# Attention weights of layer 3: scores computed twice, the second time with keys on partitions, instead of transposing the weights

## The chip, the core and the metric

The kernel runs on one core of a Trainium2 chip. The core has TensorE (PE, matmuls; its weight loads are listed as PEld), VectorE (DVE), ScalarE (ACT), GpSimd (POOL) and SyncE (SP), which here only issues DMAs. Matmul results land in PSUM, eight banks of 128 partitions by 512 fp32 numbers; everything else works from SBUF. The metric is the device time of one execution in microseconds (us), taken as the median of several runs.

## The reference

The program is a chain of four layers on 4 sequences of 512 tokens with 512 channels: a cross-attention (layer 0), two recurrent layers (1 and 2) and a perceiver-like cross-attention with an MLP (layer 3). All arithmetic is fp32. Only layer 3 is changed. There the latents are the output of layer 2, and the keys are the 512 context tokens (some masked) followed by the 512 latents:

```python
h = jnp.concatenate([x, latents], axis=1)          # 512 context tokens, 512 latents
q = (latents @ q_w + q_b).reshape(b, k_len, NH, DH)     # NH 16 heads, DH 32
kv = (h @ kv_w + kv_b).reshape(b, p + k_len, NH, DH, 2)
kmat, v = (kv[..., 0], kv[..., 1])
attn = jnp.einsum('bkhd,bnhd->bhkn', q, kmat) / DH
attn = jnp.where(full_mask[:, None, None, :], attn, -jnp.inf)
attn = jax.nn.softmax(attn.astype(jnp.float32), axis=-1)
attn_out = jnp.einsum('bhkn,bnhd->bkhd', attn, v).reshape(b, k_len, H)
attn_out = attn_out @ out_w + out_b + residual
out = rmsnorm(attn_out, postnorm_w)
out = jax.nn.gelu(out @ mlp_w1 + mlp_b1) @ mlp_w2 + mlp_b2
return out + residual
```

## The kernel before

Layer 3 goes through 4 batches (b). A batch's channels are cut into 4 blocks of 128 (m), and a block holds 4 heads of 32 channels (r). The 512 queries are cut into 4 tiles of 128 (lt). A **group** is (b, m, lt): 128 queries, 4 heads, 1024 keys; there are 64 of them. A **unit** is (b, m), four groups.

- `begin(b)` loads the context, transposed on the host, and the mask, and transposes the latents on TensorE (L1125).
- `prep(b, m)` loads the three weight blocks (L1137) and makes q (L1141, negated and divided by 32), the keys kT (L1148) for context (a = 0) and latents (a = 1), with channels on partitions, and the values v with keys on partitions (L1153). It is cut into five pieces by `yield`.
- `scores(g, a)` (L1169) makes, for one half of the keys and each head, a matmul over 32 channels with the 128 queries on the PSUM partitions and 512 keys along the row. The four heads use four row tiles of the array, so they run beside each other. A VectorE instruction (L1179) adds the mask, writes the scores to SBUF and keeps the least along the row (scores are negated, so this is the largest).
- `weights(g)`: ScalarE takes exp(least - score) and sums it along the row (L1197), VectorE inverts the sum (L1200), GpSimd multiplies the weights by it (L1201).
- `turned` transposes the weights on TensorE, four heads of 128 keys at a time (L1209), and copies them to SBUF, on VectorE for three of eight key blocks (L1212), on ScalarE for five (L1214).
- `values` multiplies v with the turned weights (L1225): 32 output rows per head, so four column tiles of the array beside each other, 128 query columns each. `attended` adds the bias of v (L1242).
- `finish(b)` is the output block of a batch: projection, residual, norm, then the MLP in 32 pieces of `ph` (first matmul and gelu) and `po` (second matmul). It has 38 pieces.

The order on TensorE in layer 3 is the program's order; the order on the other engines is made by the framework's scheduler from the dependences and tiles. The main loop (L1325) issues, for each group, the scores of this group, the transposes and values of the group before, and between them pieces of the next preparation (`early`) and of the output block of the batch before (`rest`). The output block of batch b - 1 starts with the first group of batch b that is turned, so during batch 0 there is none, and that of batch 3 runs alone at the end. PSUM is shared out as four banks for scores and pieces, two for transposes, and one for values.

A tile with a tag and `bufs=n` rotates through n buffers: a new tile waits until the readers and writers of the one n allocations before are done. DMAs on SP are issued in order, so one that waits for its buffer holds up those behind it.

Layer 0, which is not changed, already works in the manner of the new code: scores once for the largest (L242, L254), the largest taken off, scores again with keys on partitions (L279), exponential (L298), values over 512 columns (L304).

Of the kernel before, what the change touches and what calls it, by code (L numbers as in the profile page):

```python
# [30 lines left out]
def tile_xattn_rwkv_perceiver(ctx: ExitStack, tc: tile.TileContext, t: dict, out: bass.AP):  # L31
# [1055 lines left out]
    def layer3():  # L1087
# [4 lines left out]
        with (  # L1092
# [3 lines left out]
            tc.tile_pool(name="l3ps", bufs=4, space=PSUM) as ps_s,  # L1096
            tc.tile_pool(name="l3pt", bufs=2, space=PSUM) as ps_t,
# [5 lines left out]
            vb = cp.tile([P, KC], F32, name="vb")  # L1103
            nc.sync.dma_start(vb, t["L3_vb"].rearrange("(k p) -> p k", p=P))
# [6 lines left out]
            def begin(b):  # L1111

                d = st[b]
                cT = d["cT"] = bp.tile([P, KC, L], F32, tag="cT", name="cT")
                nc.sync.dma_start(cT, t["ctxT"][:, b * L : (b + 1) * L].rearrange("(k p) n -> p k n", p=P))
                mi = bp.tile([P, L], I32, tag="mi", name="mi")
                nc.sync.dma_start(mi, t["mask3"][b : b + 1, :].to_broadcast([P, L]))
                nm = d["nm"] = bp.tile([P, 2, L], F32, tag="nm", name="nm", bufs=2)
                nc.vector.tensor_scalar(nm[:, 0], mi, 0.0, 1e30, ALU.is_equal, ALU.mult)
                nc.gpsimd.memset(nm[:, 1], 0.0)  # L1120
                xT = d["xT"] = bp.tile([P, KC, L], F32, tag="xT", name="xT")
                for k in range(KC):
                    pt = ps_s.tile([P, L], F32, tag="s", name="ptx")
                    for i in range(LT):
                        nc.tensor.transpose(pt[:, i * P : (i + 1) * P], xn[b][i][:, k * P : (k + 1) * P], ident)  # L1125
                    nc.scalar.copy(xT[:, k, :], pt)
                    if k % 2:
                        yield

            def prep(b, m):  # L1130
# [4 lines left out]
                for x in "qkv":  # L1135
                    w3[x] = bp.tile([P, KC, P], F32, tag="w3" + x, name="w3" + x, bufs=2)
                    nc.sync.dma_start(w3[x], t["L3_W" + x][:, ms].rearrange("(k p) n -> p k n", p=P))  # L1137
                q = d["q", m] = bp.tile([P, L], F32, tag="q", name="q", bufs=2)
# [4 lines left out]
                kT = d["k", m] = bp.tile([P, 2, L], F32, tag="kT", name="kT", bufs=2)  # L1143
                v = d["v", m] = bp.tile([P, NB, P], F32, tag="v", name="v", bufs=2)
                for a, src in enumerate((d["cT"], d["xT"])):
                    pm = ps_s.tile([P, L], F32, tag="s", name="pk")
                    mm(pm, [(w3["k"][:, k, :], src[:, k, :]) for k in range(KC)])
                    nc.scalar.activation(kT[:, a, :], pm, AF.Identity, bias=cols[:, m, 1:2])  # L1148
                    yield
                    pm = ps_s.tile([P, LT, P], F32, tag="s", name="pv")  # L1150
                    for j in range(LT):
                        mm(pm[:, j, :], [(src[:, k, j * P : (j + 1) * P], w3["v"][:, k, :]) for k in range(KC)])
                    nc.vector.tensor_copy(v[:, a * LT : (a + 1) * LT, :], pm)  # L1153
                    yield

            def scores(g, a):

                b, m, lt = g
                d = st[b]
                if a == 0:  # L1160
                    d["mx"] = sp.tile([P, 2, NR], F32, tag="mx", name="mx", bufs=3)
                    d["sm"] = sp.tile([P, NR], F32, tag="sm", name="sm", bufs=3)
                    d["sc"] = [sp.tile([P, 2, L], F32, tag="sc", name="sc", bufs=8) for _ in range(NR)]
                mx = d["mx"]
                ps = []
                for r in range(NR):
                    rs = slice(32 * r, 32 * r + 32)
                    psc = ps_s.tile([P, L], F32, tag="s", name="psc")
                    nc.tensor.matmul(  # L1169
                        psc,  # L1170
                        d["q", m][rs, lt * P : (lt + 1) * P],
                        d["k", m][rs, a, :],
                        start=True,
                        stop=True,
                        tile_position=(32 * r, 0),
                    )
                    ps.append(psc)
                for r in range(NR):
                    nc.vector.tensor_tensor_reduce(  # L1179
                        d["sc"][r][:, a, :],  # L1180
                        ps[r],
                        d["nm"][:, a, :],
                        1.0,
                        mx[:, 0, r : r + 1] if a else 3.0e38,
                        ALU.add,
                        ALU.min,
                        mx[:, a, r : r + 1],
                    )

            def weights(g):  # L1190

                d = st[g[0]]
                mx, sm, scs = d["mx"], d["sm"], d["sc"]
                rs = sp.tile([P, NR], F32, tag="rs", name="rs", bufs=3)
                for r in range(NR):
                    sc = scs[r].rearrange("p a l -> p (a l)")
                    nc.scalar.activation(  # L1197
                        sc, sc, AF.Exp, bias=mx[:, 1, r : r + 1], scale=-1.0, accum_out=sm[:, r : r + 1]
                    )
                    nc.vector.reciprocal(rs[:, r : r + 1], sm[:, r : r + 1])  # L1200
                    nc.gpsimd.tensor_scalar(sc, sc, rs[:, r : r + 1], 0.0, ALU.mult, ALU.add)  # L1201
                return scs

            def turned(g, scs, ss, po):

                for s in ss:
                    pt = ps_t.tile([P, NR, P], F32, tag="t", name="pt")
                    for r in range(NR):
                        nc.tensor.transpose(pt[:, r, :], scs[r][:, s // LT, s % LT * P : (s % LT + 1) * P], ident)  # L1209
                    aT = sp.tile([P, NR, P], F32, tag="aT", name="aT", bufs=6)  # L1210
                    if s > 4:
                        nc.vector.tensor_copy(aT, pt)  # L1212
                    else:
                        nc.scalar.copy(aT, pt)  # L1214
                    sums.append((g, s, aT, po))

            sums = []

            def values():

                for g, s, aT, po in sums:
                    b, m, lt = g
                    v = st[b]["v", m]
                    for r in range(NR):
                        nc.tensor.matmul(  # L1225
                            po[32 * r : 32 * r + 32, :],
                            v[:, s, 32 * r : 32 * r + 32],
                            aT[:, r, :],
                            start=(s == 0),
                            stop=(s == NB - 1),  # L1230
                            tile_position=(0, 32 * r),
                        )
                    if s == NB - 1:
                        attended(g, po)
                sums.clear()

            def attended(g, po):
                b, m, lt = g
                d = st[b]
                if "y" not in d:  # L1240
                    d["y"] = bp.tile([P, KC, L], F32, tag="y", name="y")
                nc.scalar.activation(d["y"][:, m, lt * P : (lt + 1) * P], po, AF.Identity, bias=vb[:, m : m + 1])  # L1242

            def finish(b):
# [5 lines left out]
                for lt in range(LT):  # L1250
# [6 lines left out]
                    sq = sp.tile([P, C], F32, tag="sq", name="sq", bufs=1)  # L1257
# [51 lines left out]

# [6 lines left out]

            groups = [(b, m, lt) for b in range(B) for m in range(KC) for lt in range(LT)]
            first = chain(begin(0), prep(0, 0))  # L1320
            for _ in first:
                pass
            early = rest = iter(())
            old = None
            for i, g in enumerate(groups + [None]):  # L1325
                if g and g[2] == 0:
                    for _ in early:
                        pass
                    b, m, _ = g
# [4 lines left out]
                if old and old[0][1:] == (0, 0) and old[0][0] > 0:  # L1334
                    for _ in rest:
                        pass
                    rest = finish(old[0][0] - 1)
                if old:
                    po = ps_o.tile([P, P], F32, tag="o", name="po", bufs=2)
                for a in range(2):  # L1340
                    if g:
                        scores(g, a)
                    values()
                    if old:
                        turned(*old, range(4 * a, 4 * a + 2), po)
                    if piece(early, rest):
                        values()
                    piece(rest)
                    if old:
                        turned(*old, range(4 * a + 2, 4 * a + 4), po)  # L1350
                old = (g, weights(g)) if g else None
            values()
# [81 lines left out]
```

## Time and profile before

| | |
|---|---|
| median of 3 runs | 3876.62 us (3872.99 to 3885.42) |
| the profiled run, its own time | 3879.5 us |
| its span, first to last instruction | 3877.8 us |
| mean granted TensorE clock | 0.962 |
| busy PE, DVE, ACT, POOL over the span | 93%, 65%, 48%, 40% |
| first scores of layer 3 (L1169) | 2446.6 us |
| last attended values (L1242) | start at 3742.3 us |
| matmul records by line: L1169, L1209, L1225 | 1024, 2048, 4096 |

Times in the views count from the span's first instruction. A row of the costliest groups gives line, engine, operation, output <- inputs, shapes, how often (x), then the busy time, the mean duration in ns of one, and the idle time of the engine before them with what ended it. A row of the timeline gives start, duration, engine, line, operation, tiles, shape and number of records merged into it. A row of stretches gives its bounds, its length, the busy time and number of instructions of each engine, the granted clock, the DMA share and GB/s. A matmul's duration contains the passage through the array, in which the next one has already begun.

### The profile page before, as it was taken

The numbers are of one execution on the slowest core, as the hardware profiler recorded it, in microseconds if no ns is written. First come the engines' busy times: TensorE is split into PE (matmuls) and PEld (weight loads), VectorE is DVE, ScalarE is ACT, GpSimd is POOL, SyncE is SP. The second block draws the span as 40 slices with busy tenths as digits, with TensorE's granted clock in tenths as the row PEclk, the third lists the DMA queues.
The fourth block names the chain that finished last, engine by engine and source line by source line (L and its number), as shares of the span: only waits on it lengthen the run. The fifth ranks groups of instructions, "written<-read, shape, count | busy, mean of one in ns | idle before, by whom it ended". The sixth has DMA issues, their size and how long they took to land.

```text
span 3877.8 us, 60788 instructions
## 1 busy us (share of the span) xinstructions
PE 3619.7 (93%) x24256; PEld 2114.2 (55%) x24256; DVE 2526.8 (65%) x4565; ACT 1856.0 (48%) x3178; POOL 1554.1 (40%) x980
## 2 busy tenths in 40 slices
PE   9999999988999999999999976889999999999989
PEld 3333333555556665656665533555666566656656
DVE  6777777589988888888888860455434443443440
ACT  4767676434444444444444422455454445444531
POOL 4777867424444444444444432222221311221220
PEclk9999999989999999999999987999999999999999
DMA  4000000155777777777777745100122112201213
GB/s 148 23 12 23 12 9 20 57 140 131 158 169 175 172 181 175 174 168 172 168 174 174 174 115 142 43 26 15 51 84 71 51 60 88 76 31 68 69 66 124
DMA packets 187115, 386.94 MB, mean 100 GB/s; under 512 B 16528, under 2 KB 43280, under 8 KB 184784
## 3 DMA queue, kind: packets, MB, share of 16 engines
q1 hardware_dynamic: 148528, 251.45, 20.1%
q0 software_dynamic: 38304, 131.61, 18.3%
q8 instruction: 191, 3.13, 0.3%
q14 instruction: 92, 0.75, 0.1%
HBM read 247.23 MB, written 4.19 MB: 65 GB/s over the span
## 4 chain that ended last, share of the span: by engine, by line
PE 70%; DVE 14%; DMA 6%; ACT 4%; issue 3%; POOL 3%; SPq 0%; POOLq 0%; DVEq 0%; ACTq 0%
PE pm L73 10%; PE pt L1209 6%; PE pv L73 6%; PE po L73 6%; PE ph L73 6%; DMA kv<-A 5%; PE psc L242 4%; PE pst L279 4%; PE psc L1169 4%; PE po L1225 3%; PE pr L73 3%; PE po L304 3%; DVE ry L867 3%; PE pk L73 3%; DVE kv L862 2%
## 5 line engine op out<-in xcount | busy, mean ns | idle before, releaser
L1201 POOL TENSOR_SCALAR sc<-sc,rs 128x1024 f32<-128x1024 f32 x256 | 288.5, 1129 | 931.6 <-DVE rs L1200 916.0
L292 POOL TENSOR_TENSOR aT<-aT,nmT 128x1536 f32<-128x1536 f32 x124 | 428.8, 3462 | 205.7 <-ACT aT L290 182.5
L254 DVE CUSTOM_DVE_ANT_0 sc<-psc,nm 128x512 f32<-128x512 f32 x512 | 354.0, 691 | 147.6 <-PE psc L242 89.9
L867 DVE TENSOR_TENSOR ry<-kv,o_r 128x1024 f32<-128x1024 f32 x256 | 350.3, 1408 | 3.4
L1209 PE MATMUL pt<-ident,sc 128*128 128x128 f32 x2048 | 285.1, 284 | 36.2 <-ACT aT L1214 36.2
L1197 ACT ACTIVATE sc<-sc,mx 128x1024 f32<-128x1024 f32 x256 | 291.9, 1142 | 38.1 <-DVE mx L1179 34.3
L862 DVE TENSOR_TENSOR_SCAN kv<-W,kv 128x1032 f32<-128x1032 f32 x128 | 295.8, 2311 | 0.0
L1179 DVE CUSTOM_DVE_ANT_0 sc<-psc,nm,mx 128x512 f32<-128x512 f32 x256 | 179.6, 746 | 171.3 <-PE psc L1169 171.3
L1214 ACT COPY aT<-pt 128x512 f32<-128x512 f32 x320 | 173.9, 584 | 241.2 <-PE pt L1209 241.0
L1209 PEld LDWEIGHTS pt<-ident,sc 128*128 128x128 f32 x2048 | 233.2, 144 | 101.6 <-issue 54.4
L290 ACT COPY aT<-pst 128x512 f32<-128x512 f32 x372 | 196.5, 595 | 177.1 <-PE pst L279 176.6
L584 POOL DMA_DIRECT2D kv<-A x127 | 119.1, 938 | 377.0 <-DVE kv L839 373.9
L298 ACT ACTIVATE aT<-aT 128x2048 f32<-128x2048 f32 x128 | 246.7, 1929 | 5.6 <-POOL aT L292 4.8
L73 PE MATMUL po<-l_m,hT 128*128 128x512 f32 x512 | 236.9, 608 | 4.4 <-ACT hT L1295 4.4
L73 PE MATMUL ph<-nT,l_m 128*128 128x256 f32 x1024 | 235.4, 384 | 0.0
L1304 DVE TENSOR_TENSOR x<-po,x 128x512 f32<-128x512 f32 x64 | 44.1, 689 | 265.3 <-PE po L73 265.3
L279 PE MATMUL pst<-q,km 32*128 32x512 f32 x1024 | 206.2, 639 | 9.4 <-DVE mxs L254 5.8
L73 PEld LDWEIGHTS ph<-nT,l_m 128*128 128x128 f32 x1024 | 191.8, 191 | 34.2 <-issue 9.9
L833 DVE TENSOR_TENSOR A<-vr,o_k 128x1024 f32<-128x1024 f32 x128 | 155.5, 1215 | 80.7 <-DMA kv<-A 80.6
L242 PE MATMUL psc<-km,q 32*128 32x512 f32 x1024 | 198.2, 651 | 0.8 <-ACT q L223 0.8
L929 POOL TENSOR_TENSOR gn_rs<-gn_rs,mhalf 128x64 f32<-128x64 f32 x16 | 186.4, 11648 | 21.7 <-DVE gn_rs L927 21.7
L881 PE MATMUL py<-ry,k 128*32 128x512 f32 x1024 | 157.8, 631 | 38.7 <-DVE ry L867 27.3
(257 smaller groups left out, 7153.1 us busy)
## 6 DMA issues: line engine op xcount, KB each, us to landing
l_m<-in_L_W SPq DMA_DIRECT2D x64, 1024.0 KB, 5.1
kv<-A POOLq DMA_DIRECT2D x127, 516.0 KB, 7.4
L_wk<-in_L_Wk SPq DMA_DIRECT2D x16, 1024.0 KB, 7.5
L_wr<-in_L_Wr SPq DMA_DIRECT2D x16, 1024.0 KB, 7.6
L_wv<-in_L_Wv SPq DMA_DIRECT2D x16, 1024.0 KB, 5.8
L_wg<-in_L_Wg SPq DMA_DIRECT2D x16, 1024.0 KB, 7.9
L_wo<-in_L_Wo SPq DMA_DIRECT2D x64, 256.0 KB, 6.9
L_fk<-in_L_fWk SPq DMA_DIRECT2D x16, 1024.0 KB, 8.9
```

Source lines behind the costliest of these rows:

```text
L73: nc.tensor.matmul(ps, lhsT, rhs, start=(i == 0), stop=(i == len(pairs) - 1))
L242: nc.tensor.matmul(psc, d["q"][g][rs, lt * P : (lt + 1) * P], d["km"][rs, a, :], start=True, stop=True, tile_position=(32 * r, 0),)
L254: nc.vector.tensor_tensor_reduce(sc, ps[r], d["nm"][lt], 1.0, -3.0e38, ALU.add, ALU.max, mxs[:, a, lt, c : c + 1])
L279: nc.tensor.matmul(pst, d["km"][rs, a, s * P : (s + 1) * P], d["q2", a][rs, :], start=True, stop=True, tile_position=(32 * r, 0),)
L290: nc.scalar.copy(w[:, r, :], pst)
L292: nc.gpsimd.tensor_tensor(w[:, n:, :], w[:, n:, :], nmT[:, None, :].to_broadcast([P, NR - n, L]), ALU.add)
L298: nc.scalar.activation(w, w, AF.Exp)
L862: nc.vector.tensor_tensor_scan(flat(kv), flat(W[g % 2]), flat(kv), 0.0, ALU.mult, ALU.add)
L867: nc.vector.tensor_tensor(y, kv[:, 4 * h : 4 * h + 4, None, :TP].to_broadcast([P, 4, 2, TP]), d["r"][:, i].rearrange("p (o m) -> p o m", o ...
L1197: nc.scalar.activation(sc, sc, AF.Exp, bias=mx[:, 1, r : r + 1], scale=-1.0, accum_out=sm[:, r : r + 1])
L1201: nc.gpsimd.tensor_scalar(sc, sc, rs[:, r : r + 1], 0.0, ALU.mult, ALU.add)
L1209: nc.tensor.transpose(pt[:, r, :], scs[r][:, s // LT, s % LT * P : (s % LT + 1) * P], ident)
```

## The change

Scores are made twice. `least` does the first pass as before, but keeps only the least of each row; the scores go to a scratch tile that nobody reads. When all four query tiles of a unit are through, `spread` transposes the column of least values, broadcast to 128 columns, so that each lands along the row on all partitions, and ScalarE copies it to `mb`. `turned` makes the scores again with operands exchanged: 128 keys on partitions, all 512 queries along the row. VectorE subtracts `mb` (it adds no mask), ScalarE takes the exponential of four heads at once, with the mask as a bias per partition. GpSimd adds the eight weight tiles of a unit up in `acc`; `counted` multiplies `acc` by ones, which sums over keys and repeats the sum on the 32 rows of the head, and VectorE inverts it. `values` works on 512 query columns; its result is copied to y, and `divided` multiplies it by the inverted sum. The bias of v is added to v itself.

```diff
-            tc.tile_pool(name="l3ps", bufs=4, space=PSUM) as ps_s,
-            tc.tile_pool(name="l3pt", bufs=2, space=PSUM) as ps_t,
+            tc.tile_pool(name="l3ps", bufs=7, space=PSUM) as ps_s,
...
-                mi = bp.tile([P, L], I32, tag="mi", name="mi")
+                mi = sp.tile([P, L], I32, tag="sc", name="mi")
                 nc.sync.dma_start(mi, t["mask3"][b : b + 1, :].to_broadcast([P, L]))
...
+                mci = bp.tile([P, LT], I32, tag="mci", name="mci", bufs=2)
+                nc.sync.dma_start(mci, t["mask3"][b].rearrange("(s p) -> p s", p=P))
+                mc = d["mc"] = bp.tile([P, LT], F32, tag="mc", name="mc", bufs=2)
+                nc.vector.tensor_scalar(mc, mci, 0.0, -1e30, ALU.is_equal, ALU.mult)
...
-                    w3[x] = bp.tile([P, KC, P], F32, tag="w3" + x, name="w3" + x, bufs=2)
+                    w3[x] = bp.tile([P, KC, P], F32, tag="w3" + x, name="w3" + x)
...
+            def row_scores(lhsT, rhs, name):
+                ps = []
                 for r in range(NR):
                     rs = slice(32 * r, 32 * r + 32)
+                    psc = ps_s.tile([P, L], F32, tag="s", name=name)
+                    nc.tensor.matmul(psc, lhsT[rs], rhs[rs], start=True, stop=True, tile_position=(32 * r, 0))
                     ps.append(psc)
+                return ps
...
+                ps = row_scores(d["q", m][:, lt * P : (lt + 1) * P], d["k", m][:, a, :], "psc")
                 for r in range(NR):
+                    sc = sp.tile([P, L], F32, tag="sc", name="sc", bufs=2)
                     nc.vector.tensor_tensor_reduce(
...
+            def spread(u):
+                b, m = u
+                d = st[b]
+                mb = d["mb"] = sp.tile([P, NR, L], F32, tag="mb", name="mb", bufs=1)
                 for r in range(NR):
+                    pb = ps_s.tile([P, L], F32, tag="s", name="pb")
+                    for lt in range(LT):
+                        nc.tensor.transpose(
+                            pb[:, lt * P : (lt + 1) * P], d["mx", m][:, 1, lt, r : r + 1].to_broadcast([P, P]), ident
                         )
+                    nc.scalar.copy(mb[:, r, :], pb)
+
+            def turned(u, s):
+                b, m = u
+                d = st[b]
+                ps = row_scores(d["k", m][:, s // LT, s % LT * P : (s % LT + 1) * P], d["q", m], "pst")
+                w = d["w", s] = sp.tile([P, NR, L], F32, tag="aT", name="aT", bufs=3)
+                for r in range(NR):
+                    nc.vector.tensor_tensor(w[:, r, :], ps[r], d["mb"][:, r, :], ALU.subtract)
+                wf = w.rearrange("p r l -> p (r l)")
+                if s < LT:
+                    nc.scalar.activation(wf, wf, AF.Exp, bias=d["mc"][:, s : s + 1], scale=-1.0)
+                else:
+                    nc.scalar.activation(wf, wf, AF.Exp, scale=-1.0)
+                if s == 1:
+                    acc = d["acc", m] = sp.tile([P, NR, L], F32, tag="acc", name="acc", bufs=1)
+                    nc.gpsimd.tensor_tensor(acc, d["w", 0], w, ALU.add)
+                elif s > 1:
+                    nc.gpsimd.tensor_tensor(d["acc", m], d["acc", m], w, ALU.add)
...
+            def counted(u):
+                b, m = u
+                d = st[b]
+                pn = ps_s.tile([P, L], F32, tag="s", name="pn")
+                columns(pn, lambda r: ones, d["acc", m], start=True, stop=True)
+                rs = d["rs", m] = sp.tile([P, L], F32, tag="sc", name="rs")
+                nc.vector.reciprocal(rs, pn)
+
+            def divided(u):
+                b, m = u
+                d = st[b]
+                y = d["y"][:, m, :]
+                nc.vector.tensor_tensor(y, y, d["rs", m], ALU.mult)
```

`columns` is the loop over four heads with column tiles that `values` had. The squares' scratch in `finish` (sq) moves to the tag sc as well. The loop runs over 138 steps, eight to a unit: in a step stand one `least` (of 8) of unit n, one `turned` (of 8) of unit n - 1, and one `values`, two steps behind its `turned`:

```diff
+            LAG = 2
...
+                w, ws = divmod(i - NB - LAG, NB)
...
+                if u:
+                    least(u, s // 2, s % 2)
+                if piece(early):
+                    pass
+                elif piece(rest):
+                    left -= 1
                 if old:
+                    if s == 0:
+                        spread(old)
+                if ws == NB - 1 and 0 <= w < len(units):
+                    counted(units[w])
+                if old:
+                    turned(old, s)
+                if left > min(34, behind(i)) and piece(rest):
+                    left -= 1
+                if 0 <= w < len(units):
+                    values(units[w], ws)
+                    if ws == NB - 1:
+                        divided(units[w])
```

A step takes a piece of the next preparation if there is one, else one of the output block; `behind(i)` says how many output pieces may still be left at step i, so that the 38 pieces are spread over the 32 steps of the next batch. An output block starts when its batch's first following unit reaches `values` (steps 42, 74 and 106).

## The prediction

> **What bounds the kernel now.** I read the page's row of 40 slices first, then the stretches of layer 3, then TensorE's order in time. Layer 3's first scores start at 2446.6 us; the last copy of attended values (L1242) is at 3742.3, and the 136 us after it, to the end at 3877.8, are the last batch's output block, which the diff hardly touches. So the change plays in 1296 us. Those I cut at 2707, where batch 0's attention ends: until then no output block of an earlier batch exists to fill gaps.
>
> ```profile
> 2446.60:2707.00 260.40, 234.69 (x2211) 149.53 (x2211) 139.55 (x403) 137.79 (x251) 76.92 (x69) 0.95 0.07 21
> 2707.00:3742.60 1035.60, 1006.10 (x7626) 646.46 (x7625) 446.08 (x1223) 508.15 (x883) 234.15 (x213) 0.98 0.19 64
> ```
>
> Columns: stretch, length, then busy time of PE, PEld, DVE, ACT, POOL, then the granted clock, DMA share and GB/s. PE is busy 97% of the second stretch and 90% of the first; VectorE (DVE) 43% and 54%. A busy PE can still wait inside its matmuls, so what a matmul run costs is read from the distance to the next run's start:
>
> ```profile
> 3161.89 1.04 PE L1209 MATMUL pt<-ident,sc 128*128 128x128 f32 x8
> 3162.86 1.25 PE L1169 MATMUL psc<-kT,q 32*128 32x512 f32 x8
> ...
> 2571.84 1.14 PE L1169 MATMUL psc<-kT,q 32*128 32x512 f32 x8
> 2572.91 0.65 PE L1225 MATMUL po<-aT,v 128*32 128x128 f32 x16
> 2573.49 1.09 PE L1209 MATMUL pt<-ident,sc 128*128 128x128 f32 x8
> ...
> 326.32 1.34 PE L279 MATMUL pst<-q,km 32*128 32x512 f32 x8
> 327.60 1.06 PE L304 MATMUL po<-aT,vp 128*32 128x512 f32 x8
> 328.59 1.14 PE L242 MATMUL psc<-km,q 32*128 32x512 f32 x8
> ```
>
> Each line is a run: start, length, line, tiles, records (two for an fp32 matmul, one for a transpose). Costs by distance: four head scores (8 records) 1.07 us, eight transposes 0.97, two value steps (16 records of 128 columns) 0.57. The last three lines are layer 0, which already works as the new code will: values over 512 columns (8 records) cost 1.00, scores with keys on partitions 1.28 here and 1.07 where nothing waits (the shortest of L279's runs, the usual one of L1169's).
>
> **TensorE's sum before.** A group (b, m, lt) is 2 score runs, 4 transpose runs, 4 value runs: 2.14 + 3.88 + 2.28 = 8.3 us; 64 groups, 531. Beside them lie 15 preparations (q, two k, two v: 3 x 3.53 + 2 x 3.67 = 17.9) 269, three batch starts 13, and three output blocks of 131 us (36 runs of 3.54, and transposes), 394. Sum 1207 of 1296: 89 us of stall and throttled clock, some 50 of them in the first stretch. There, and nearly everywhere, TensorE sets the pace.
>
> **What TensorE does after.** Per unit (b, m), four groups:
> - *Removed:* 16 transpose runs, 15.5 us, and 16 value runs, 9.1.
> - *Kept:* 8 score runs (least), 8.6.
> - *Added:* 8 runs of turned scores at 1.07, 8.6; 8 value runs of 512 columns at 1.00, 8.0; 16 transposes in spread, 1.9; the count against ones, like a value run, 1.0.
>
> That is 28.1 against 33.2: 5.1 saved, x 16 = **82 us**, all on the engine that binds. Sum after: 1207 - 82 = 1125. What is late next is VectorE.
>
> **VectorE.** The rows:
>
> ```profile
> L1179 DVE CUSTOM_DVE_ANT_0 sc<-psc,nm,mx 128x512 f32<-128x512 f32 x256 | 179.6, 746 | 171.3 <-PE psc L1169 171.3
> L1214 ACT COPY aT<-pt 128x512 f32<-128x512 f32 x320 | 173.9, 584 | 241.2 <-PE pt L1209 241.0
> L298 ACT ACTIVATE aT<-aT 128x2048 f32<-128x2048 f32 x128 | 246.7, 1929 | 5.6 <-POOL aT L292 4.8
> L292 POOL TENSOR_TENSOR aT<-aT,nmT 128x1536 f32<-128x1536 f32 x124 | 428.8, 3462 | 205.7 <-ACT aT L290 182.5
> ```
>
> Instructions overlap by some 0.08 us, so back to back a score reduction costs 0.61 to 0.67 and a 128x512 copy or add out of PSUM 0.60. Per unit: 32 reductions 20.5, kept. Gone: 12 copies L1212 (7.3) and 16 small reciprocals (1.3). New: 32 subtractions (priced by L288, 0.686 long) 19.3; one product 0.7; one reciprocal of 128x512, which has no row. Between the 128x1 (163 ns) and 128x16 (248 ns) reciprocals lie 85 ns for 15 elements, so 512 would be 3.1 us; the ends are 0.6 (a copy's pace) and 5. I take 3.1. With two v adds 1.3, VectorE goes from 30 to **45 us per unit**.
>
> Here the Trainium skill speaks against the change: "TensorEngine Tiling (Array Packing)", Performance Considerations (PSUM Bottleneck), says that tiling speeds up the matmuls but not emptying PSUM, which can become the limit, and that ScalarE and VectorE should share it. Before, 20 of a unit's 32 transposed tiles left by ScalarE; after, all 32 leave by VectorE. If VectorE bound throughout, 15 us more x 16 less the 82 saved would make it 158 us slower. The trace says otherwise for the filled stretch: 446 us busy of 1036, plus about 12 x 15 = 180, is 626 of some 1000. In the unfilled stretch, TensorE needs 28.1 + 17.9 = 46 per unit and VectorE 45: two engines at one height. There I expect no more than a small gain.
>
> **ScalarE and GpSimd** stay under. ScalarE per unit: 8 exponentials of 1.93, four spread copies 0.58, q, k and y: 21 us instead of 36; more table loads between gelu and exponential (31 and 30 now, perhaps 32 per output block, 1.28 each) are 41 us per batch and have room in some 330. GpSimd: 7 adds of 128x2048, by L292's 2.25 ns per element 4.6 us, 32 per unit instead of 18; cover: three weight tiles, so that an add has until the third next step, 20 us and more; without it each step would wait for its add.
>
> A second rule against it: "SBUF — State Buffer" (Who interferes with whom) says a VectorE instruction with two SBUF inputs is blocked for the whole of a GpSimd instruction that reads SBUF. The subtractions read one operand from PSUM, and layer 0's reductions keep 691 ns beside a GpSimd busy two thirds of the time. Only the product in divided has two: 0.7 by row, up to 5.3 by the rule, once per unit. By the rule that is 4 x 4.6 = 18 us in unfilled units and nothing behind output work; I take 0 to 18, within the stalls below.
>
> **Steps that move.** A unit is now 8 steps, values 2 behind, so the first output block starts at step 42 instead of after 17 groups. mi shares the two sc slots with the reductions' scratch: its load can no longer be issued early. SP waits at it for a reduction of the same step, with mci and later weight loads queued behind; VectorE's mask instruction waits for the landing (4.2 us for mi), with reductions behind it. Three times, 0 to 6 us each: 10 in all. The w3 tiles lose their second buffer, but their readers finish 3 steps before the next unit's, 20 us or more against a landing of 2.8: nothing. rs and sq in the same slots hold a reduction for about 1 us per unit: within the stalls.
>
> **Stalls after.**
> - Steps 0 to 7, scores only: 4 us.
> - Steps 8 to 41, 34 without output work. Layer 0's runs, by mean distance, cost 1.36 (scores), 1.54 (turned) and 1.02 (values) against 1.07, 1.07, 1.00: 0.78 us lost per step, at VectorE's 76% busy. Here VectorE is fuller: 1.2, with 0.78 and 2.2 as ends. 34 x 1.2 = 41.
> - Steps 42 to 137: output pieces lie between every two score runs, as now. Today's loss there, 39 us on 997 of work (3.9%), on the 898 left (1125 less 27 and 200 for the steps before) is 35; ends 2% (18) and 8% (72).
> - mi: 10.
>
> Sum 90, as before (89). So the forecast is the matmul sum alone: 1296 - 82 + 1 gives 1215 and a span of 3877.8 - 81 = 3797. The profiled run took 3879.5 around its span of 3877.8, 0.1% over the median 3876.6; the same step from the median is **3795 us**.
>
> **Rivals.**
> 1. *Stalls shrink too.* Seven PSUM buffers in one pool instead of four and two, and pieces paced evenly; the trace has 25 us of transposes waiting for copies in the first stretch. Stalls 18 + 14 + 4: 3741. Against: VectorE is fuller.
> 2. *VectorE paces the unfilled steps and slows the rest.* 34 x 2.2 + 72 + 4 + 10 = 161, 71 more than I take: 3866. At half of that, 3830. For: the PSUM rule; against: 35% room in filled steps.
> 3. *Slower: TensorE, in order, stands at each step before the turned scores until VectorE frees PSUM tiles.* The price is a stall per step over all 138 steps; it decides from (1296 - 1125) / 138 = 1.24 us. At 1.5 it is 207 us of stall: 3913. For: layer 0 loses 0.78 in just this way. Against: layer 0's steps last 5.9 us, filled steps here over 9, and 3.5 us of other matmuls stand between the two score runs.
> 4. *It does not free TensorE:* turned scores cost layer 0's 1.54 by nature, not by waiting: 8 x 0.47 x 16 = 60 of 82 lost, 3855. Against: the same form runs at 1.07 where nothing waits.
>
> Chances: forecast 0.52, rival 1 0.18, rival 2 (with 4) 0.23, rival 3 0.07. A measurement of this kernel tells no change from about 0.3%, 3865 to 3888. Faster 0.89, same 0.04, slower 0.07. Range 3738 to 3850: down to rival 1, up to the middle of rivals 2 and 4.
>
> **What would show it.** Right: the last y copy near 3660; turned runs 1.1 us apart from what follows in filled steps; VectorE near 60% busy there and over 80% until the first output block; no transposes of weights. Wrong: turned or psc runs of 1.5 us and more beside output pieces (rivals 2, 3), a reciprocal over 5 us, GpSimd adds over 7 us, or TensorE idle at the head of a unit waiting for mb or acc.

## The result and the profile after

The changed kernel takes 3847.68 us (median of 5 runs, 3840.83 to 3856.98) against 3876.62: 29 us less, a ratio of 0.9926 (95% interval 0.9902 to 0.9950). That is inside the stated range, close to its upper end, and about a third of the 82 us that were forecast. The profiled run took 3843.51 us around a span of 3841.5.

Layer 3's first scores start at 2444.8, the first output piece (pout) at 2718.3, and the last values end at 3703.5; then the last output block runs alone, as before. The stretches between them, with the columns of the stretches shown of before:

```profile
2444.80:2718.30 273.50, 271.42 (x1498) 125.72 (x1497) 218.79 (x502) 92.28 (x79) 128.99 (x29) 0.98 0.07 22
2718.30:3703.50 985.20, 944.56 (x4629) 458.87 (x4625) 606.57 (x1221) 389.59 (x389) 399.56 (x108) 0.98 0.21 68
```

The first stretch, without output pieces, took what was forecast (273.5 us; the forecast came to 272 up to step 42, whose early part also lies ahead of the first pout). The second took 985 where 933 were forecast. VectorE is busy 80% in the first and 62% in the second, also as forecast. TensorE in a dense part of the second:

```profile
3004.17 1.14 PE L1175 MATMUL pst<-q,kT 32*128 32x512 f32 x8
3005.24 1.06 PE L1235 MATMUL po<-aT,v 128*32 128x512 f32 x8
3006.23 1.14 PE L1175 MATMUL psc<-kT,q 32*128 32x512 f32 x8
3007.30 3.72 PE L73 MATMUL ph<-nT,l_m 128*128 128x256 f32 x16
3010.96 1.14 PE L1175 MATMUL pst<-q,kT 32*128 32x512 f32 x8
```

Turned scores and scores cost 1.07 from start to start, values 0.99: the prices taken from layers 0 and 3. Only the output run, 3.66 where such a run took 3.56 before, is a little dearer. So where nothing waits the sum is right but for this, and most of the missing 50 us must be waits. The groups that answer to those shown of before:

```profile
L1230 POOL TENSOR_TENSOR acc<-acc,aT 128x2048 f32<-128x2048 f32 x96 | 435.0, 4531 | 420.4 <-ACT aT L1225 235.6
L1220 DVE TENSOR_TENSOR aT<-pst,mb 128x512 f32<-128x512 f32 x512 | 317.4, 681 | 132.0 <-PE pst L1175 132.0
L1189 DVE CUSTOM_DVE_ANT_0 sc<-psc,zeros,mx 128x512 f32<-128x512 f32 x256 | 177.5, 746 | 50.7 <-PE psc L1175 48.4
L1225 ACT ACTIVATE aT<-aT 128x2048 f32<-128x2048 f32 x64 | 122.3, 1911 | 196.6 <-DVE aT L1220 191.6
```

Each duration is within 2% of the row it was taken from (4.6, 0.686, 0.746, 1.93). No engine got more work than was counted.

**Where the time stands.** I laid each TensorE run's distance to the next beside its undisturbed cost. Before, the first stretch lost 42 us and the second 58; after, 42 and 105. The undisturbed costs themselves fell by some 82 to 85 us, as forecast (82). Of the 105, 14 are the dearer output and preparation runs; the rest is not spread: most steps lose 0.1 to 0.2 us, but the first five of each output block lose about 14 together, and single steps later 4 to 7. Two places show why. The first is in step 44, during the pout pieces; VectorE, then GpSimd, then TensorE, in order of time:

```profile
2737.29 0.68 DVE L1189 CUSTOM_DVE_ANT_0 sc<-psc,nm 128x512 f32<-128x512 f32 x1
2737.90 0.09 DVE L1189 DVE_READ_ACCUMULATOR2_ANT mx<- 128x1 f32 x1
2742.37 0.49 DVE L1286 TENSOR_SCALAR ao<-ao,rms 128x512 f32<-128x512 f32 x1 [4.39 <-POOL rms L79]
2742.78 0.68 DVE L1189 CUSTOM_DVE_ANT_0 sc<-psc,nm 128x512 f32<-128x512 f32 x1
```

```profile
2736.08 4.53 POOL L1230 TENSOR_TENSOR acc<-acc,aT 128x2048 f32<-128x2048 f32 x1 [6.50 <-ACT aT L1223]
2740.57 1.26 POOL L1287 TENSOR_TENSOR x<-x,b 128x512 f32<-128x512 f32 x1
2741.79 0.55 POOL L79 TENSOR_TENSOR rms<-rms,mhalf 128x1 f32<-128x1 f32 x1
```

```profile
2740.29 1.14 PE L1175 MATMUL pst<-q,kT 32*128 32x512 f32 x8
2743.52 3.70 PE L73 MATMUL pout<-l_wo,y 128*128 128x512 f32 x8 [2.09 <-DVE mx L1189]
```

The power (inverse square root) of the norm is taken on GpSimd from an argument that VectorE had written by 2737.4 (L78). GpSimd's power (L79, 0.55 us) is queued behind an addition of 4.53, which had just begun, and a bias of 1.26. VectorE's next instruction (L1286) needs the power, so VectorE stands 4.39 us with two of four score tiles unread in PSUM. TensorE then finds no free PSUM tile for pout and stands 2.09. Over layer 3, the last output block included, this wait grew from the first line below (before) to the second (after); columns: waiter, releaser, us in total, times, longest.

```profile
DVE ao L1261 <- POOL rms L79: 7.3, 7, 1.4
```

```profile
DVE ao L1286 <- POOL rms L79: 36.4, 13, 5.0
```

The second place is where a unit ends, here in step 58: VectorE, then GpSimd.

```profile
2892.33 4.70 DVE L1267 TENSOR_TENSOR y<-y,rs 128x512 f32<-128x512 f32 x1 [2.28 <-ACT y L1252]
2896.95 0.68 DVE L1189 CUSTOM_DVE_ANT_0 sc<-psc,nm 128x512 f32<-128x512 f32 x1
```

```profile
2891.97 4.51 POOL L1228 TENSOR_TENSOR acc<-aT 128x2048 f32<-128x2048 f32 x1 [16.74 <-ACT aT L1223]
```

The product of y and the inverted sum reads two tiles of SBUF. It takes 4.70 us instead of 0.68 and ends 0.55 us after the addition that had begun just before it. Eight of the sixteen products are stretched so, to 2.6 or 4.7, and each ends 0.55 or 0.56 us after its addition; none before the first output piece, where no GpSimd instruction runs beside them.

One more VectorE instruction of the output block reads two SBUF tiles, the addition of the residual (L1281). Before, it never took more than 0.69 us; now it is stretched twice, in the second and in the third block, and again ends 0.55 us after a GpSimd addition. VectorE, then GpSimd:

```profile
3083.32 4.16 DVE L1281 TENSOR_TENSOR ao<-ao,x 128x512 f32<-128x512 f32 x1
```

```profile
3082.41 4.52 POOL L1230 TENSOR_TENSOR acc<-acc,aT 128x2048 f32<-128x2048 f32 x1 [6.50 <-ACT aT L1223]
```

### The profile page after: what moved, and what is told of

The parts are those of the page before. It is cut to its first block, busy times and chain, and to the rows that moved or that the text cites. A ratio compares the mean times of both kernels' runs of the same rounds, so it can differ in the third digit from the quotient of the medians.

```text
span 3841.5 us, 52407 instructions
## 1 busy us (share of the span) xinstructions
PE 3589.6 (93%) x20544; PEld 1900.9 (49%) x20544; DVE 2765.4 (72%) x4665; ACT 1691.6 (44%) x2514; POOL 1768.4 (46%) x834
## 4 chain that ended last, share of the span: by engine, by line
PE 64%; DVE 15%; DMA 6%; issue 5%; POOL 5%; ACT 5%; SPq 0%; POOLq 0%; DVEq 0%; ACTq 0%
PE pm L73 9%; PE pv L73 6%; PE po L73 5%; DMA kv<-A 5%; PE ph L73 5%; PE psc L242 5%; PE pst L279 4%; PE pst L1175 3%; PE psc L1175 3%; PE po L304 3%; PE pr L73 3%; DVE ry L867 3%; PE pk L73 3%; PE po L1235 2%; DVE kv L862 2%
## 5 line engine op out<-in xcount | busy, mean ns | idle before, releaser
L1230 POOL TENSOR_TENSOR acc<-acc,aT 128x2048 f32<-128x2048 f32 x96 | 435.0, 4531 | 420.4 <-ACT aT L1225 235.6
L254 DVE CUSTOM_DVE_ANT_0 sc<-psc,nm 128x512 f32<-128x512 f32 x512 | 354.0, 691 | 147.0 <-PE psc L242 89.3
L1220 DVE TENSOR_TENSOR aT<-pst,mb 128x512 f32<-128x512 f32 x512 | 317.4, 681 | 132.0 <-PE pst L1175 132.0
L298 ACT ACTIVATE aT<-aT 128x2048 f32<-128x2048 f32 x128 | 246.7, 1929 | 5.7 <-POOL aT L292 4.9
L1228 POOL TENSOR_TENSOR acc<-aT 128x2048 f32<-128x2048 f32 x16 | 72.4, 4524 | 327.6 <-ACT aT L1223 327.6
L1189 DVE CUSTOM_DVE_ANT_0 sc<-psc,zeros,mx 128x512 f32<-128x512 f32 x256 | 177.5, 746 | 50.7 <-PE psc L1175 48.4
L1225 ACT ACTIVATE aT<-aT 128x2048 f32<-128x2048 f32 x64 | 122.3, 1911 | 196.6 <-DVE aT L1220 191.6
L1223 ACT ACTIVATE aT<-aT,mc 128x2048 f32<-128x2048 f32 x64 | 128.2, 2003 | 180.3 <-DVE aT L1220 171.0
L1189 DVE CUSTOM_DVE_ANT_0 sc<-psc,nm 128x512 f32<-128x512 f32 x256 | 162.9, 686 | 46.5 <-PE psc L1175 45.0
```

Source lines behind the costliest of these rows:

```text
L254: nc.vector.tensor_tensor_reduce(sc, ps[r], d["nm"][lt], 1.0, -3.0e38, ALU.add, ALU.max, mxs[:, a, lt, c : c + 1])
L298: nc.scalar.activation(w, w, AF.Exp)
L1189: nc.vector.tensor_tensor_reduce(sc, ps[r], d["nm"][a], 1.0, mx[:, 0, lt, r : r + 1] if a else 3.0e38, ALU.add, ALU.min, mx[:, a, lt, r : ...
L1220: nc.vector.tensor_tensor(w[:, r, :], ps[r], d["mb"][:, r, :], ALU.subtract)
L1230: nc.gpsimd.tensor_tensor(d["acc", m], d["acc", m], w, ALU.add)
```

## The experiments

The theory after this reading (A): the loss beside output work is VectorE standing for GpSimd, at these two places. Its rival (B) is the one of the prediction: VectorE, now the only engine that empties the score tiles, is simply too full.

A difference from the changed kernel is taken below from the two ratios to the kernel before; by their intervals it is good to some 13 us. What an edit is worth is therefore read from the profiles too, by the second stretch, from the first output piece to the last values (985.2 us in the changed kernel); layers 0 to 2, which no edit touches, differ by up to 18 us among these profiles.

**Product from PSUM.**

```diff
-                    nc.scalar.copy(d["y"][:, m, :], d["po"])
...
-                nc.vector.tensor_tensor(y, y, d["rs", m], ALU.mult)
+                nc.vector.tensor_tensor(d["y"][:, m, :], d["po"], d["rs", m], ALU.mult)
```

> The product with the inverted sums reads the attended values from PSUM instead of from a copy in SBUF (the ScalarE copy goes). Theory A: the product takes 0.69 us each of 16 times instead of 0.7 to 4.7, the long steps in mid-batch (5.9, 7.0 and twice 4.2 us lost) shrink to under 1.5, time 15 to 25 us under the changed kernel, about 3827. Theory B: within 5 us of it.

3817.05 us, ratio 0.9837 (0.9815 to 0.9859): 0.9% below the changed kernel, some 34 us. Its row of products, and its second stretch, 26 us shorter:

```profile
L1265 DVE TENSOR_TENSOR y<-po,rs 128x512 f32<-128x512 f32 x16 | 10.9, 684 | 0.2
```

```profile
2710.10:3669.00 958.90, 927.23 (x4629) 452.21 (x4625) 585.18 (x1221) 384.14 (x378) 397.94 (x108) 0.98 0.21 70
```

All sixteen take 0.68 to 0.69; in the changed kernel the row was 32.4 us busy and 14.3 idle ahead of it. Steps 58, 67, 90 and 99 lose 0.1 to 0.2 us each. VectorE has the same number of instructions, and the steps that lost time with a stretched product no longer lose it, so B's forecast fails here. The edit takes away two things at once, the stretching (21.5 us of VectorE) and the wait for ScalarE's copy (14.3); it does not say how much each was worth to TensorE.

**Norm one piece later.** In `finish`, the multiplication by the rms (L1286) was issued after the `yield`.

> In the output block the multiplication of a row tile by its rms is issued one piece later, so that VectorE need not stand for GpSimd's power instruction. Theory A: VectorE's wait for rms falls from 33 us to under 8, the loss in the first five steps of the three output blocks from 43 us to about 10, time about 3815. Theory B: the loss stays, since TensorE waits for PSUM tiles that VectorE is too busy to free; 3840 to 3850.

3847.28 us, ratio 0.9910 (0.9879 to 0.9941): no change. But VectorE's order is the scheduler's in this layer, and it had put the instruction back in the same place: the wait is again 36.4 us in 13 times. The run tested nothing about A; it says that moving a line of the program is no way to move an instruction on an engine that the program does not order.

**Values before the turned scores.** The three lines of `values` and `divided` were moved above `turned(old, s)`.

> Within a step the values come before the turned scores, so that the preparation or output piece is followed by a column-tiled matmul and not by a row-tiled one. If the 0.1 us by which every piece of full matmuls grew (3.54 to 3.63) is the change from the full array to row tiles: about 120 of them go, 10 to 12 us less, 3836. If it belongs to the pieces themselves (chip, clock), they stay at 3.63 and the time at 3848. The values read weights that are one turned step younger; if these are late, TensorE waits for the exponential and it is slower.

3873.01 us, ratio 0.9979 (0.9967 to 0.9991): slower than the changed kernel by 0.5%. Pieces followed by column-tiled values still cost 3.63, so the added 0.1 us is not due to row tiles. In both kernels it goes with what follows: 3.53 to 3.54 ahead of transposes or of values over 128 columns, 3.63 ahead of tiled matmuls over 512 columns (before, two pieces ahead of scores cost 3.63 too). Why is open. The slowing is told by the order of TensorE:

```profile
2607.12 1.14 PE L1175 MATMUL pst<-q,kT 32*128 32x512 f32 x8
2608.09 2.13 PE L1175 MATMUL psc<-kT,q 32*128 32x512 f32 x8
2610.15 3.70 PE L73 MATMUL pk<-cT,w3k 128*128 128x512 f32 x8
```

With no values between them, the next scores follow the turned ones at once, eight tiles for seven PSUM buffers, and cost 2.06 instead of 1.07. This happens in 61 steps, against ten where turned scores follow scores in the changed kernel; the values hardly wait for the exponential (0.8 us in all). Here is the wait of the prediction's third rival; the order chosen in the change keeps one run between and mostly avoids it.

**One addition in place of seven.**

```diff
-                    nc.gpsimd.tensor_tensor(acc, d["w", 0], w, ALU.add)
-                elif s > 1:
-                    nc.gpsimd.tensor_tensor(d["acc", m], d["acc", m], w, ALU.add)
+                    nc.gpsimd.tensor_tensor(acc, w, plus[:, None, :].to_broadcast([P, NR, L]), ALU.add)
```

> Leaves out the summing of the weights: per unit one GpSimd addition (a constant 1 to the second weight tile) stands for the seven, so the divisor is not the softmax sum; TensorE, VectorE and ScalarE do what the changed kernel does. Theory A (GpSimd's additions hold up VectorE): loss of TensorE from the first output piece to the last y copy falls from 105 us to about 50, VectorE's wait for rms to under 8 us, time about 3795. Theory B (VectorE is too full as the only engine that empties the scores' PSUM tiles): within 10 us of the changed kernel, 3838 to 3858.

A first form, which kept the addition of the first two weight tiles and left out the other six, gave no time: its inverted sums were not finite. The form shown took 3808.92 us, ratio 0.9814 (0.9793 to 0.9836): 1.1% below the changed kernel, 43 us. Its second stretch is 35 us shorter, and its loss falls from 105 to 71, not to the 50 expected. Why is in two lines, the wait for rms and the products:

```profile
DVE ao L1286 <- POOL rms L79: 3.3, 4, 1.0
```

```profile
L1267 DVE TENSOR_TENSOR y<-y,rs 128x512 f32<-128x512 f32 x16 | 32.2, 2012 | 14.0 <-ACT y L1252 13.9
```

The first wait is nearly gone, and with it the loss of the first four steps of each output block (0.1 to 0.2 us per step, bar one). The products are stretched as before: the one addition left, in the second step of a unit, is the very one that meets them. A single GpSimd instruction per unit, in the wrong step, is enough to stretch them.

**Norm on ScalarE.**

```diff
-                    nc.vector.tensor_scalar(ao, ao, rstd, None, ALU.mult)
+                    nc.scalar.activation(ao, ao, AF.Identity, scale=rstd)
```

> Only the multiplication of a row tile by its rms moves, from VectorE to ScalarE, which then does the standing for GpSimd's power instruction. Theory A: the loss in the first five steps of the three output blocks, 43 us, falls to 10 to 15; the long steps in mid-batch stay; time about 3817. Theory B: no more than 4 us (12 instructions of 0.4 us less on VectorE).

3817.98 us, ratio 0.9835 (0.9815 to 0.9855): 35 us below the changed kernel. GpSimd does all it did; the engine that stands has changed:

```profile
ACT ao L1286 <- POOL rms L79: 58.9, 16, 5.9
```

The second stretch is 22 us shorter, at 10 us less of VectorE:

```profile
2711.40:3674.70 963.30, 941.25 (x4628) 457.52 (x4624) 596.54 (x1209) 397.38 (x401) 400.45 (x108) 0.98 0.21 69
```

The first five steps of the output blocks lose 20 us instead of 42, and the long steps in mid-batch stay. ScalarE stands longer than VectorE did, 58.9 us, and little comes of it: no PSUM tile of the scores waits for ScalarE, and TensorE's transposes of ao wait for it 8.4 us in all, as they did for VectorE (9.1). The residual additions shifted too, so that none stands for a sum of weights any more (three take 1.16); their share of the 22 is not separated.

**Both.**

> The product from PSUM and the multiplication by rms on ScalarE together. If the two losses are separate places they add up: 31 us and 25 to 30 us off the changed kernel, about 3790, and TensorE's loss beside output work falls to about 45 us, what the prediction had. If both are one backlog of VectorE, the second brings less than 10.

3782.51 us, ratio 0.9748 (0.9728 to 0.9768): some 69 us below the changed kernel, 98 below the kernel before. Its stretches:

```profile
2441.90:2715.60 273.70, 271.71 (x1497) 126.59 (x1496) 219.50 (x502) 89.95 (x75) 130.54 (x29) 0.98 0.07 22
2715.60:3644.10 928.50, 914.92 (x4629) 446.59 (x4625) 575.19 (x1209) 391.94 (x390) 400.62 (x108) 0.99 0.22 72
```

The first stretch is the same to 0.2 us, the second 56.7 us shorter: the whole effect lies beside output work, at 575 us of VectorE instead of 607, most of that difference being the stretched products. Alone, the two edits took 26 and 22 us off this stretch; together they take somewhat more than the sum, so they are two places and not one backlog. Its loss is now 49 us: 14 of the dearer runs and 35 that were not looked into.

**Reciprocal replaced by a copy**, on top of both (`tensor_copy(rs, pn)`).

> On top of the two, the reciprocal (3.36 us, 16 times) is replaced by a copy of 0.69 us, so the values are multiplied by the sum instead of divided. If what is left is VectorE standing at the joints, 16 x 2.7 = 43 us of VectorE time go and up to 15 us of the time, most of it in the steps before the first output block; if the reciprocal lies beside matmuls, under 5.

3770.53 us, ratio 0.9719 (0.9696 to 0.9742): 11 us less, of the 43 us of VectorE time that went, with intervals that overlap. By the profiles 7.6 us of the gain lie in the first stretch, where 11 us of VectorE time went, and 1.9 in the second, where 28 went. Beside output work the reciprocal lies mostly beside matmuls; before the first output piece it is one more moment at which VectorE stands while PSUM tiles fill.

**Mask row in its own buffer**, on top of both (`mi` from the pool `bp` with its own tag).

> On top of the product from PSUM and the norm on ScalarE, the mask row mi has its own buffer again, so its load is issued early. The prediction gave that wait 10 us. If so, time about 3773; if VectorE's 5 us stand beside matmuls that have PSUM tiles left, 2 to 4 us and within the noise of 3782.

3787.98 us, ratio 0.9753 (0.9738 to 0.9767): nothing. The changed kernel's VectorE waits for this load 8.7 us in three times after the first scores (a fourth wait lies ahead of them); here it does not wait, and TensorE gains nothing by it.

**More matmul**, on top of both: `columns(pn, ..)` in `counted` four times over.

> On top of the product from PSUM and the norm on ScalarE, the count against ones is made four times over in the same PSUM tile: 3 runs of 1.0 us more for each of 16 units, 48 us of TensorE, nothing else. If TensorE's matmul sum sets the time throughout, as the prediction has it, 48 us more, 3830; if VectorE sets it until the first output block (4 of the 16 counts), about 36; if VectorE sets it everywhere, under 15.

3824.18 us, ratio 0.9845 (0.9829 to 0.9861): about 38 us more. The stretches give it more sharply:

```profile
2449.60:2734.00 284.40, 282.05 (x1594) 130.77 (x1593) 219.52 (x502) 89.95 (x75) 130.66 (x29) 0.98 0.07 21
2734.00:3695.20 961.20, 947.63 (x4917) 457.59 (x4913) 574.30 (x1209) 391.84 (x390) 400.58 (x108) 0.99 0.21 70
```

By the distances of the pn runs 9.4 us were added in the first stretch and 32.9 in the second (0.88 for a further run on average, not the 1.0 that the expectation took). The stretches grew by 10.7 and 32.7. Matmul time passes to the total one for one, also before the first output piece, where the expectation's middle case had VectorE set the pace. Since 7.6 of 11 us of the reciprocal's time pass to the total there as well, neither engine alone sets the pace in that stretch.

## Why the prediction was wrong

*The matmul sum* (5.1 us per unit, 82 in all) was right as a difference: the undisturbed costs of the runs fell by 82 to 85, and the last experiment shows that such time counts in full. The sum itself was some 12 us too high: run by run, the work of before comes to 1195 us, not 1207.

*The stretch before output work*, which I held to be the doubtful one, came out at the forecast 273 us, with VectorE at 80%. Its loss is 42 us, where 45 were taken. That is in part luck: the 1.2 us per step was a guess between 0.78 and 2.2, and by steps the loss is uneven, 0.1 where a preparation piece stands between and nothing waits, 1.3 to 1.9 in steps without one, 2 to 5 around the start of a unit. The rule on PSUM bottlenecks from the Trainium skill's "TensorEngine Tiling (Array Packing)", Performance Considerations (PSUM Bottleneck), was weighed rightly for the load: that all score tiles leave by VectorE did not make its busy time the limit. What TensorE loses it still loses waiting for VectorE to empty PSUM, at single moments.

*Durations* were near: reciprocal 3.36 (3.1 taken), additions 4.53 (4.6), subtractions 0.681 (0.686).

*The step that failed* is the third term of "Stalls after": for steps 42 to 137 it carried today's share of loss over, 3.9%, "35; ends 2% (18) and 8% (72)", and of the blocked product it said that it cost "nothing behind output work". The loss there was 105 us. The starting share was misread as well: from 2707 to 3742.6 the kernel before lost 58 us on 977 of work (6%), not 39 on 997. With the two edits together the stretch is 928.5 us, where 933 were forecast (898 + 35), but that match is luck: it is 879 of work and 49 of loss. What the edits took away is 57 us. The share could not be carried over, because the change puts 4.5 us instructions on GpSimd, and two VectorE instructions wait for GpSimd there:
- The power of the norm. I gave GpSimd's load (32 us per unit) and concluded that it "stays under". What mattered was not its load but the length of one instruction ahead of a short one, for which VectorE, in its own order, stands. The row of before (7.3 us of waits for rms) was there to be asked: what is queued ahead of L79 now? Moving the wait to ScalarE was worth 22 us of the stretch.
- The product. The rule of the Trainium skill's "SBUF — State Buffer" (Who interferes with whom), that a VectorE instruction with two SBUF inputs contends with a GpSimd instruction that reads SBUF, was cited with its price, 5.3 us; the trace agrees, with up to 4.71. I placed it in the unfilled steps, where none was blocked, and dismissed it beside output work, where eight were. Together with the wait for y ahead of it, it was worth 26 us of the stretch. "Only the product in divided has two" SBUF inputs was wrong as well: the residual addition of the output block has them too.

Common to both is that 38% idle VectorE does not help when it stands at a moment when TensorE has seven PSUM tiles and no more. Beside output work a step with a stop of 4 to 5 us loses 2 to 7 on TensorE.

*The smaller terms.* The wait for mi, 10 us in the forecast, is worth nothing that can be measured. Every preparation and output run before tiled matmuls of 512 columns takes 0.1 us longer (3.63 for 3.54), some 14 us in the second stretch, which the sum put at nothing; the swapped order showed only that row tiles are not the cause.

Of the rivals, 4 came nearest to the time (3855) and is out: turned scores cost 1.07 where nothing waits. Rival 2 (3830 at half, 3866) had the right place, VectorE beside output work, for the wrong reason, a VectorE too full. Rival 3's wait exists in nearly half of the steps of the swapped order, in few of this one.

## What to carry to other kernels

When a change loads an engine that has room, look for the short instructions that share its queue and ask who stands for them: their delay can now be as long as the instructions ahead (here up to 5 us), and it counts if the one who stands is the one who frees PSUM. Give such a wait to an engine that frees no score tiles (here ScalarE, which stood 59 us at little cost), and look through all VectorE instructions beside a busy GpSimd for those with two SBUF operands: let one operand come from PSUM where it can. With both, the changed kernel gives 3782.51 us, 0.9748 of the kernel before.

## What was not expected of the hardware

A reciprocal of 128x512 fp32 from PSUM takes 3.36 us, five times a copy of that shape (0.69). A VectorE product with two SBUF operands stretches from 0.68 to 4.71 us beside a GpSimd addition. All stretched ones end 0.55 us after the addition, however early they started, so the standing lies inside the recorded duration: it shows as a long instruction and in no view of waits. Four runs of the same column-tiled matmul in a row cost 3.57 us, 0.86 for each further one, where a single one between other tilings costs 1.00.
